# Windows of 64 nodes per octet, dst compared on two halves of the array, and 124 columns copied per octet in a graph-network kernel

## The chip, the cores and the metric

The kernel runs on one core of one Trainium2 chip. The metric is the device time of one execution in microseconds; the time of a version is the median of several runs. The profile is one execution taken by the hardware profiler. Its engines are PE (TensorE: matmuls; PEld is its weight load), DVE (VectorE), ACT (ScalarE), POOL (GpSimd) and SP (SyncE, which here only issues DMAs). Each engine runs its own instructions in order; they meet through semaphores.

## The reference

A message-passing layer on 12,500 nodes of 64 features and 400,000 edges, sorted by their target `dst`, followed by a residual and a layer norm. All arithmetic is float32.

```python
m_in = concatenate([x[src], x[dst], edge_attr])       # 64 + 64 + 16
h = silu(m_in @ W1 + b1)
messages = silu(h @ W2 + b2)
agg = segment_sum(messages, dst, num_segments=12500)
out = silu(concatenate([x, agg]) @ W3 + b3)
result = layernorm(x + out)
```

## The kernel before

**Tiles, octets, chunks.** The edges are cut into 3125 tiles of 128. Eight tiles make an octet (391 of them, the last with five tiles), three octets a chunk (131). The loop at L555 runs over octets and spreads each octet's work over several of its turns. Inside it the order of instructions on PE, ACT, DVE and SP is the order of the text (`manual_schedule`, L552); POOL has only the gathers.

**First layer.** The product `x @ W1[0:64]` is computed once for all nodes and written to the table `pa` in DRAM (`table`, L171, in turns 1 to 5 of the loop). The rows of `pa` for an octet's sources are gathered in three ways:

- by POOL's indirect DMA, one per tile of 128 edges (`gather`, L332, line L341), three octets ahead, into one of five buffers `ga`. The first nine octets (`RAW`) gather rows of `x` itself, because the table is not there yet;
- by copies of single columns. `x` transposed is resident in SBUF (`xs`, two copies on two halves of the partitions). For one pair of tiles in some octets (`pairs`), ACT and DVE copy 256 columns of 64 features one by one (`columns`, L244, line L267), each a copy of 64 x 4 bytes whose address is a register that was loaded from the list of sources. The copies are spread over the turns before: 56 per octet on ACT (`ACOLS`, two halves of 28, registers in loads of at most 16) and 48 on DVE (`VCOLS`, two halves of 24, one load each). 104 per octet replace a pair of tiles, two gathers, every 2.46 octets: 153 pairs in all;
- by single-row DMAs from SP (`rows`, L280), 16 per octet: 23 pairs.

The rest of the first layer uses that edges are sorted: the targets of a chunk lie in a window of 112 nodes from its first `dst` on. `window_load` (L346) reads these nodes' columns of `x`, `window_product` (L354) multiplies them with `W1[64:128]`, `window_copy` (L359) puts the result into rows 0 to 111 of the weights `xw`, whose last 16 rows hold the attributes' part of `W1`. `load` (L365) broadcasts an octet's `dst` to 112 partitions (`dr`) and loads the edges' attributes into the last 16 rows of `oh`; `compare_dst` (L377) writes into the first 112 rows of `oh` whether an edge's `dst` is the node of the row. One product of `xw` and `oh` (L401) so gives the target's and the attributes' part; even and odd tiles go to the two halves of the columns of the array. The gathered rows are added by products with the identity (L415), the copied columns by a product with `W1` (L412). ACT applies silu (L419).

**Second layer and sums.** `second_layer` (L422) multiplies with `W2` (L428 for the bias, L430) and applies silu (L434). `compare_nodes` (L385) makes, per tile, the matrix of which edge belongs to which of the 112 nodes, and `add_up` (L437) multiplies the messages with it (L443), accumulating over a chunk's 24 tiles in PSUM. `add_window` (L446) adds the sum to `agg` in SBUF, once a chunk.

**Nodes.** When the windows have passed a group of 512 nodes, `node_product` to `store` (L467 to L510) compute the output, spread over later turns by the table `todo`.

**Check.** After the loop (L612 to L635) DVE computes the distance of each `dst` from its window's base and whether any lies outside; if so, the slow version `general` runs. It does not for these inputs.

Of the kernel before, what the change touches and what calls it, by code (L numbers as in the profile page):

```python
# [20 lines left out]
P = 128  # L21
G = 4
CT = 24
OT = 8
W = 112
# [4 lines left out]
ACOLS = (28, 28)  # L30
VCOLS = (24, 24)
ROWS = 16
ALOAD = 16
XBASE = (0, 64 << 18)
XADDR = 35840
# [8 lines left out]
def kernel(  # L44
# [8 lines left out]
    attr_t: bass.AP,  # L53
    base: bass.AP,
# [31 lines left out]
    with ExitStack() as inner:  # L86
        windows(inner, tc, ident, badi, pa, x, xt, src_c, src_row, dst_c, dst_row, attr_t, base, w1, b1, w2, b2, w3, b3, out, edges)
# [7 lines left out]
def windows(ctx, tc, ident, badi, pa, x, xt, src_c, src_row, dst_c, dst_row, attr_t, base, w1, b1, w2, b2, w3, b3, out, edges):  # L95
# [5 lines left out]
    NCH = base.shape[1]  # L101
    assert W + A == P and N + W <= NP
# [15 lines left out]
    bi = fast.tile([1, NCH], I32, name="bi")  # L118
# [48 lines left out]
    def resident(s, c):  # L167
        w = min(XC, NP - c)
        nc.sync.dma_start(xs[s * D:(s + 1) * D, c:c + w], xt[:, c:c + w])
# [19 lines left out]
    bf = fast.tile([1, NCH], F32, name="bf")  # L189
    nc.vector.tensor_copy(bf, bi)  # L190
    rowi = fast.tile([P, W], I32, name="rowi")
    nc.gpsimd.iota(rowi, pattern=[[1, W]], base=0, channel_multiplier=0)
    row = fast.tile([P, W], F32, name="row")
    nc.vector.tensor_copy(row, rowi)
    coli = fast.tile([P, 1], I32, name="coli")
    nc.gpsimd.iota(coli, pattern=[[0, 1]], base=0, channel_multiplier=1)
    colf = fast.tile([P, 1], F32, name="colf")
    nc.vector.tensor_copy(colf, coli)

    wb = fast.tile([P, NCH], F32, name="wb")  # L200
    wps = ctx.enter_context(tc.tile_pool(name="wps", bufs=1, space=PSUM))
    wrow = wps.tile([P, 512], F32, name="wrow")
    wn = wrow[:, 3 * W:3 * W + NCH]
    assert 3 * W + NCH <= 512
    pb = mis.tile([P, NCH], F32, name="mm")
    nc.tensor.matmul(pb, ones, bf, start=True, stop=True)
    nc.vector.tensor_copy(wb, pb)
    nc.vector.tensor_scalar(wn, pb, colf, None, op0=OP.add)

    xw = []  # L210
    for k in range(3):
        t = fast.tile([P, D], F32, name=f"xw{k}")
        nc.sync.dma_start(t[W:P, :], w1[2 * D:2 * D + A, :])
        xw.append(t)

    octs = []
    for c in range(NCH):
        t1 = min(TILES, (c + 1) * CT)
        octs += [(c, t, min(OT, t1 - t), t == c * CT, t + OT >= t1) for t in range(c * CT, t1, OT)]

    with tc.tile_pool(name="gat", bufs=AHEAD + 2) as gat, tc.tile_pool(name="drp", bufs=2) as drp, \
            tc.tile_pool(name="hot", bufs=3) as hot, \
            tc.tile_pool(name="ehp", bufs=4) as ehp, \
            tc.tile_pool(name="work", bufs=2) as work, tc.tile_pool(name="win", bufs=2) as win, \
# [19 lines left out]
        def columns(o, eng, part):  # L244
# [3 lines left out]
            if eng == ENG.Activation:  # L248
                lo, n, copy = lo + sum(ACOLS[:part]), ACOLS[part], nc.scalar.copy
            else:  # L250
                lo, n, copy = lo + sum(ACOLS) + sum(VCOLS[:part]), VCOLS[part], nc.vector.tensor_copy
            hi = lo + n
            while lo < hi:
# [3 lines left out]
                n = min(hi - lo, P - e0 % P, ALOAD if eng == ENG.Activation else P)  # L257
# [8 lines left out]
                for e, r in zip(range(e0 % P, e0 % P + n), regs):  # L266
                    copy(t[h, 4 * e:4 * e + 4], xb[h, ds(r - (XBASE[s] + XADDR), 4)])  # L267
# [62 lines left out]
        sums = psa.tile([P, 2, W], F32, name="pg")  # L330
# [15 lines left out]
        def window_load(c):  # L346
            regs = nc.values_load(bi[0:1, c:c + 1], engines=(ENG.SP, ENG.DVE), min_val=0, max_val=N - 1,
                                  skip_runtime_bounds_check_because="dst names a node")
            winreg[c] = regs
            xr = win.tile([D, W], F32, name="xr")  # L350
            nc.sync.dma_start(xr, xt[:, ds(regs, W)])
            winrow[c] = xr

        def window_product(c):  # L354
            pw = mis.tile([P, D], F32, name="mm")
            nc.tensor.matmul(pw[0:W, :], winrow[c], w1ab[:, 1, :], start=True, stop=True)  # L356
            winrow[c] = pw

        def window_copy(c):  # L359
            nc.vector.tensor_copy(xw[c % 3][0:W, :], winrow[c][0:W, :])  # L360
            r = wrow[:, c % 3 * W:(c % 3 + 1) * W]
            nc.vector.tensor_scalar(r, row, wb[:, c:c + 1], None, op0=OP.add)
            winrow[c] = r

        def load(o):  # L365
            c, t0, n, first, last = octs[o]
            n2 = n + n % 2
            e = slice(t0 * P, (t0 + n2) * P)
            dr = drp.tile([W, OT * P], I32, name="dr")
            nc.sync.dma_start(dr[:, :n2 * P], dst_row[:, e].to_broadcast([W, n2 * P]))  # L370
            oh = hot.tile([P, OT * P], F32, name="oh")
            nc.sync.dma_start(oh[W:P, :n2 * P], attr_t[:, e])
            loaded[o] = dr, oh
# [3 lines left out]
        def compare_dst(o):  # L377
            c, t0, n, first, last = octs[o]
            n2 = n + n % 2
            dr, oh = loaded.pop(o)  # L380
            nc.vector.tensor_tensor(oh[0:W, :n2 * P], dr[:, :n2 * P], wn[0:W, c:c + 1].to_broadcast([W, n2 * P]),  # L381
                                    op=OP.is_equal)
            hots[o] = [oh]

        def compare_nodes(o):  # L385
            c, t0, n, first, last = octs[o]
            eh = ehp.tile([P, OT, W], F32, name="eh")
            nc.vector.tensor_tensor(eh[:, :n], winrow[c][:, None, :].to_broadcast([P, n, W]),  # L388
                                    dc[:, t0:t0 + n, None].to_broadcast([P, n, W]), op=OP.is_equal)
            hots[o].append(eh)  # L390

        def first_layer(o):
# [6 lines left out]
            ohv = oh.rearrange("p (i s e) -> p s i e", s=2, e=P)  # L399
            for s in range(2):  # L400
                nc.tensor.matmul(p1[s * D:(s + 1) * D, :k], xw[c % 3], ohv[:, s, :k], start=True, stop=False,  # L401
# [35 lines left out]
        def add_up(o):  # L437
            c, t0, n, first, last = octs[o]
            m, eh = made.pop(o)
            pg = sums[:, c % 2, :]  # L440
            for i in range(n):
                s = i % 2
                nc.tensor.matmul(pg[s * D:(s + 1) * D, :], m[:, i, :], eh[:, i, :],  # L443
                                 start=(first and i < 2), stop=(last and i >= n - 2), skip_group_check=True)

        def add_window(c):  # L446
            a = agg[:, ds(winreg[c], W)]
            nc.vector.tensor_tensor(a, a, sums[:, c % 2, :], op=OP.add)  # L448
# [8 lines left out]
        eps = nv.tile([P, 1], F32, name="eps")  # L457

# [59 lines left out]
        NO = len(octs)  # L518
# [8 lines left out]
        for q in range(early):  # L527
            o = lead[due[q]] + 2
# [3 lines left out]
            later(o + 1, node_stats, q)  # L532
        for q0 in range(0, rest, RB):
            o = lead[due[q0 + RB - 1]] + 2
            later(o + 2, root, q0, q0 + RB)
            later(o + 3, inverse, q0, q0 + RB)
            for r in range(RB):
                later(o + 3 + 2 * r, divide, q0 + r)
                later(o + 4 + 2 * r, store, q0 + r)
# [6 lines left out]
        load(0)  # L546
        load(1)
        tables = list(range(0, N, 4 * P))
        per = -(-len(tables) // TABLES)
        parts = list(range(0, NP, XC))  # L550

        with tc.manual_schedule(engines={ENG.PE, ENG.Activation, ENG.DVE, ENG.SP}):  # L552
            compare_dst(0)
            compare_nodes(0)
            for o in range(NO + 1):  # L555
# [9 lines left out]
                if o == 8:  # L565
                    nc.sync.dma_start(dc[:, SCT:], dst_c[:, SCT:])
# [12 lines left out]
                if o + 2 < NO:  # L579
                    load(o + 2)  # L580
                    if octs[o + 2][3]:
                        window_load(octs[o + 2][0])
# [3 lines left out]
                if o >= 3 and octs[o - 3][4]:  # L586
                    add_window(octs[o - 3][0])
# [316 lines left out]
```

## Time and profile before

| | |
|---|---|
| median of 3 runs | 3553.34 us (3553.28 to 3558.27) |
| profiled execution | 3555.16 us, span of its instructions 3553.3 us |
| span per octet | 9.09 us |
| mean TensorE clock granted | 0.752 of full |
| L341, gathers on POOL | 2701 from `pa`, 72 from `x` |
| L267, column copies | 21112 on ACT (188 ns each, overlapping), 18056 on DVE (204 ns) |
| DMA | 327 MB, 92 GB/s in the mean |

In the groups below a line reads: source line, engine, operation, output <- inputs by the program's names, shape, count | busy us, mean ns of one | idle us of the engine just before them, and what ended most of that idle time. "issue" is time for which the profile shows nothing that the engine waits for. A line of the timeline gives start and duration in us, engine, line, operation, and in brackets the idle time before it. A line of waits gives who waited for whom, us in total, times, and the longest.

### The profile page before, as it was taken

How to read it: one execution, taken by the hardware profiler on the slowest of the kernel's cores; microseconds unless marked ns; L12 is line 12 of the kernel's file. 1: busy time of each engine (PE TensorE's matmuls, PEld its weight loads, DVE VectorE, ACT ScalarE, POOL GpSimd, SP SyncE). 2: the span in 40 equal slices, each digit the busy share in tenths (PEclk: the TensorE clock that was granted, in tenths of full speed). 3: DMA queues.
4: the chain of work that ended last, by engine and by line, in shares of the span. 5: the costliest groups of instructions: out<-in, count | busy, mean ns of one | idle time of the engine just before them, and what ended most of it. 6: DMA issues, size and time to landing. Idle time of an engine off the chain costs nothing.

```text
span 3553.3 us, 96997 instructions
## 1 busy us (share of the span) xinstructions
PE 2717.1 (76%) x15387; PEld 1796.0 (51%) x15387; DVE 2551.0 (72%) x19955; ACT 2598.8 (73%) x21941; POOL 2659.2 (75%) x2782
## 2 busy tenths in 40 slices
PE   7877877777777778777777777777877777777786
PEld 5554554555545455455454554544544545545454
DVE  3667767777687677776777777777778777677673
ACT  1568777787787777777877777778778777777772
POOL 7677777777777777777777777777777777777774
PEclk7867777777777777777777777777677777777776
DMA  6433333333333333333333333333333333333331
GB/s 158 131 90 95 86 89 92 84 92 90 88 99 91 91 89 85 95 86 89 96 93 94 91 85 93 91 89 89 86 95 94 90 92 86 91 90 87 90 95 47
DMA packets 199259, 327.19 MB, mean 92 GB/s; under 512 B 94959, under 2 KB 103306, under 8 KB 197722
## 3 DMA queue, kind: packets, MB, share of 16 engines
q1 hardware_dynamic: 96142, 226.51, 20.3%
q0 software_dynamic: 88736, 91.04, 13.8%
q10 hardware_dynamic: 13740, 3.32, 0.4%
q14 instruction: 511, 4.19, 0.4%
q8 instruction: 130, 2.13, 0.3%
HBM read 314.20 MB, written 6.40 MB: 90 GB/s over the span
## 4 chain that ended last, share of the span: by engine, by line
POOL 50%; issue 20%; DMA 17%; PE 12%; ACT 1%; DVE 0%; SPq 0%; ACTq 0%; POOLq 0%; DVEq 0%
POOL ga L341 50%; DMA ga<-pa,sc 16%; PE p L430 3%; PE pg L443 2%; PE p L401 2%; PE p L415 1%; PE mm L177 1%; PE p L428 1%; ACT cx L267 1%; PE mm L477 1%; PE mm L476 1%; DMA ga<-in_x,sc 0%; PE p L410 0%; PE p L412 0%; PE mm L406 0%
## 5 line engine op out<-in xcount | busy, mean ns | idle before, releaser
L341 POOL DMA_INDIRECT ga<-pa,sc x2701 | 2589.9, 959 | 838.8 <-issue 746.9
L267 ACT COPY cx<-xs 64x4 uint8 x21112 | 2079.2, 188 | 216.8 <-issue 172.0
L267 DVE COPY cx<-xs 64x4 uint8 x18056 | 1458.6, 204 | 204.4 <-issue 172.7
L415 PE MATMUL p<-ident,ga 128*128 128x128 f32 x2702 | 616.8, 349 | 784.2 <-DMA ga<-pa,sc 781.4
L415 PEld LDWEIGHTS p<-ident,ga 128*128 128x128 f32 x2702 | 461.4, 233 | 1109.6 <-issue 945.6
L430 PE MATMUL p<-w2d,h 128*128 128x128 f32 x3126 | 621.9, 361 | 0.0
L419 ACT ACTIVATE h<-p,b1s 128x512 f32<-128x512 f32 x391 | 268.2, 686 | 480.6 <-PE p L415 437.4
L430 PEld LDWEIGHTS p<-w2d,h 128*128 128x128 f32 x3126 | 530.0, 256 | 127.0 <-issue 127.0
L401 PE MATMUL p<-oh,xw 128*64 128x512 f32 x1564 | 561.8, 806 | 5.5 <-DMA sc<-in_src_c 5.5
L388 DVE TENSOR_TENSOR eh<-wrow,dc 128x896 f32<-128x896 f32 x391 | 424.7, 1086 | 178.9 <-PE pg L443 165.3
L443 PE MATMUL pg<-eh,m 128*64 128x112 f32 x6250 | 528.5, 329 | 14.0 <-ACT m L434 13.9
L381 DVE TENSOR_TENSOR oh<-dr,wrow 112x1024 f32<-112x1024 int32 x391 | 473.1, 1210 | 28.2 <-DMA dr<-in_dst_row 16.8
L443 PEld LDWEIGHTS pg<-eh,m 128*64 128x64 f32 x6250 | 420.3, 178 | 83.5 <-issue 42.4
L434 ACT ACTIVATE m<-p 128x512 f32<-128x512 f32 x391 | 232.6, 595 | 116.2 <-PE p L430 83.0
L428 PE MATMUL p<-b2r,one 3*128 3x512 bf16 x391 | 190.3, 487 | 0.0
L360 DVE COPY xw<-mm 112x64 f32<-112x64 f32 x131 | 29.0, 222 | 208.5 <-PE mm L356 208.5
L448 DVE TENSOR_TENSOR agg<-agg,pg 128x112 f32 x131 | 35.0, 267 | 193.5 <-PE pg L443 184.8
L412 PEld LDWEIGHTS p<-cx,w1d 128*128 128x128 f32 x306 | 56.7, 233 | 188.6 <-issue 188.6
L401 PEld LDWEIGHTS p<-oh,xw 128*64 128x64 f32 x1564 | 94.0, 165 | 60.3 <-issue 23.7
L483 ACT ACTIVATE z<-mm 128x256 f32<-128x256 f32 (+1 forms) x25 | 9.6, 383 | 115.3 <-PE mm L477 115.3
L412 PE MATMUL p<-cx,w1d 128*128 128x128 f32 x306 | 91.3, 388 | 0.0
L341 POOL DMA_INDIRECT ga<-in_x,sc x72 | 68.1, 946 | 22.7 <-issue 20.6
(73 smaller groups left out, 790.2 us busy)
## 6 DMA issues: line engine op xcount, KB each, us to landing
dr<-in_dst_row SPq DMA_DIRECT2D x390, 448.0 KB
rx<-pa SPq DMA_DIRECT2D x5888, 0.2 KB
ga<-pa,sc POOLq DMA_INDIRECT x2701
oh<-in_attr_t SPq DMA_DIRECT2D x390, 64.0 KB
xs<-in_xt SPq DMA_DIRECT2D x12, 512.0 KB
xr<-in_xt SPq DMA_DIRECT2D x131, 28.0 KB
pa<-v ACTq DMA_DIRECT2D x24, 128.0 KB
xa<-in_x SPq DMA_DIRECT2D x24, 128.0 KB
```

What stands on the lines that cost most here:

```text
L267: copy(t[h, 4 * e:4 * e + 4], xb[h, ds(r - (XBASE[s] + XADDR), 4)])
L341: nc.gpsimd.indirect_dma_start(out=ga[:, i, :], out_offset=None, in_=x if o < RAW else pa[:, :], in_offset=bass.IndirectOffsetOnAxis(ap=sc ...
L381: nc.vector.tensor_tensor(oh[0:W, :n2 * P], dr[:, :n2 * P], wn[0:W, c:c + 1].to_broadcast([W, n2 * P]), op=OP.is_equal)
L388: nc.vector.tensor_tensor(eh[:, :n], winrow[c][:, None, :].to_broadcast([P, n, W]), dc[:, t0:t0 + n, None].to_broadcast([P, n, W]), op=OP. ...
L401: nc.tensor.matmul(p1[s * D:(s + 1) * D, :k], xw[c % 3], ohv[:, s, :k], start=True, stop=False, skip_group_check=True)
L412: nc.tensor.matmul(p1[:, 0, :], w1d, cols.pop(o), start=False, stop=False, skip_group_check=True)
L415: nc.tensor.matmul(p1[:, i, :], g2.rearrange("p s d -> p (s d)"), ident, start=False, stop=(i == k - 1), skip_group_check=True)
L419: nc.scalar.activation(h[:, :k], p1[:, :k], AF.Silu, bias=b1s)
L428: nc.tensor.matmul(p2[:, :n2, :], one3, b2r[:, :n2, :], start=True, stop=False, skip_group_check=True)
L430: nc.tensor.matmul(p2[:, 2 * i:2 * i + 2, :].rearrange("p s d -> p (s d)"), h[:, i, :], w2d, start=False, stop=(i == k - 1), skip_group_ch ...
L434: nc.scalar.activation(m[:, :n2], p2[:, :n2], AF.Silu)
L443: nc.tensor.matmul(pg[s * D:(s + 1) * D, :], m[:, i, :], eh[:, i, :], start=(first and i < 2), stop=(last and i >= n - 2), skip_group_chec ...
```

## The change

Each octet gets a window of its own, of 64 nodes for the first layer (`W`) and 48 for the sums (`S`). `base` holds the first `dst` of each octet. Window load, product, copy and add therefore run once per octet; the base registers are loaded for four octets at a time (`bases`); the product stands at the head of a turn, before the first layer, and the add one turn later than before. The product is written to both halves of the partitions, so `xw` holds the 64 nodes twice.

`dst` and attributes are arranged on the host (`dst_2`, `attr_2`): even tiles in the upper half of the partitions, odd tiles in the lower. `load` brings a chunk's `dst` with two broadcasts and its attributes with one DMA. `compare_dst` then runs over 128 partitions x 512 elements. The first layer's product is split: one product of the attributes (32 partitions) with the block-diagonal `w1c`, and two products of 64 x 64 quadrants of the array, even tiles on one, odd tiles on the other.

For the node compare, `dc` is turned in place into the distance from the octet's base (`relative`), in pieces during the loop; one row `row` of 0 to 47 serves all octets. The check's minimum and maximum are taken in ten pieces from turn 30 on; at the end only small steps are left, with `evi` written into `xs`.

Columns: ACT 32 and 28 per octet, DVE 32 and 32. Registers come in loads of 16 and then 8. DVE's copy is written as a `tensor_reduce` with maximum over one element. The resident copies of `x` and the late part of `dst` are loaded from ACT's queue instead of SP's.

```diff
-W = 112
+W = 64
+S = 48
-ACOLS = (28, 28)
-VCOLS = (24, 24)
+ACOLS = (32, 28)
+VCOLS = (32, 32)
-ALOAD = 16
+LOADS = (16, 8)
...
     def resident(s, c):
         w = min(XC, NP - c)
-        nc.sync.dma_start(xs[s * D:(s + 1) * D, c:c + w], xt[:, c:c + w])
+        nc.scalar.dma_start(xs[s * D:(s + 1) * D, c:c + w], xt[:, c:c + w])
...
+    rel = dc.bitcast(F32)
+
+    def relative(a, b):
+        f = b // OT * OT
+        if f > a:
+            nc.vector.tensor_tensor(rel[:, a:f].rearrange("p (c t) -> p c t", t=OT),
+                                    dc[:, a:f].rearrange("p (c t) -> p c t", t=OT),
+                                    wb[:, a // OT:f // OT, None].to_broadcast([P, (f - a) // OT, OT]), op=OP.subtract)
...
                 for e, r in zip(range(e0 % P, e0 % P + n), regs):
-                    copy(t[h, 4 * e:4 * e + 4], xb[h, ds(r - (XBASE[s] + XADDR), 4)])
+                    to, frm = t[h, 4 * e:4 * e + 4], xb[h, ds(r - (XBASE[s] + XADDR), 4)]
+                    if eng == ENG.DVE:
+                        nc.vector.tensor_reduce(to, frm[:, :, None], AX.X, OP.max)
+                    else:
+                        nc.scalar.copy(to, frm)
...
-        def window_product(c):
+        def window_product(o):
             pw = mis.tile([P, D], F32, name="mm")
-            nc.tensor.matmul(pw[0:W, :], winrow[c], w1ab[:, 1, :], start=True, stop=True)
-            winrow[c] = pw
+            for q in range(2):
+                nc.tensor.matmul(pw[q * W:(q + 1) * W, :], winrow[o], w1ab[:, 1, :], start=True, stop=True)
+            winrow[o] = pw
...
-            nc.vector.tensor_tensor(oh[0:W, :n2 * P], dr[:, :n2 * P], wn[0:W, c:c + 1].to_broadcast([W, n2 * P]),
-                                    op=OP.is_equal)
+            oh = hot.tile([P, OT // 2 * P], F32, name="oh")
+            e = o % 3 * OT // 2 * P
+            w = n2 // 2 * P
+            nc.vector.tensor_tensor(oh[:, :w], dr[:, e:e + w], wn[:, o:o + 1].to_broadcast([P, w]), op=OP.is_equal)
...
-            for s in range(2):
-                nc.tensor.matmul(p1[s * D:(s + 1) * D, :k], xw[c % 3], ohv[:, s, :k], start=True, stop=False,
+            h = slice(o % 3 * 2 * A, (o % 3 + 1) * 2 * A)
+            nc.tensor.matmul(p1[:, :k], w1c[h, :], loaded[c][1][h, :k * P], start=True, stop=False, skip_group_check=True)
+            for q in range(2):
+                h = slice(q * W, (q + 1) * W)
+                nc.tensor.matmul(p1[q * D:(q + 1) * D, :k], xw[o % 3][h, :], oh[h, :k * P], start=False, stop=False,
                                  skip_group_check=True)
...
-            pg = sums[:, c % 2, :]
+            pg = sums[:, o % 4, :]
             for i in range(n):
                 s = i % 2
                 nc.tensor.matmul(pg[s * D:(s + 1) * D, :], m[:, i, :], eh[:, i, :],
-                                 start=(first and i < 2), stop=(last and i >= n - 2), skip_group_check=True)
+                                 start=(i < 2), stop=(i >= n - 2), skip_group_check=True)
...
-                if o + 2 < NO:
-                    load(o + 2)
-                    if octs[o + 2][3]:
-                        window_load(octs[o + 2][0])
+                if o + 2 < NO and octs[o + 2][3] and o + 2:
+                    load(octs[o + 2][0])
+                if o + 3 < NO:
+                    window_load(o + 3)
+                if o + 1 < NO:
+                    window_product(o + 1)
                 if o + 1 < NO:
                     compare_dst(o + 1)
                 columns(o, ENG.DVE, 0)
-                if o >= 3 and octs[o - 3][4]:
-                    add_window(octs[o - 3][0])
+                if o >= 4:
+                    add_window(o - 4)
...
-        evi = nv.tile([P, NCH], I32, name="evi")
-        nc.gpsimd.iota(evi, pattern=[[STEP, NCH]], base=0, channel_multiplier=0)
-        lag = xs[:, TILES:TILES + NCH]
-        nc.vector.tensor_tensor(lag, evi, wb, op=OP.subtract)
+        evi = xs.bitcast(I32)[:, :3 * NCH]
+        nc.gpsimd.iota(evi, pattern=[[STEP, NCH], [0, 3]], base=0, channel_multiplier=0)
+        lag = xs[:, 3 * NCH:3 * NCH + NO]
+        nc.vector.tensor_tensor(lag, evi[:, :NO], wb, op=OP.subtract)
```

## The prediction

> **What bounds the kernel now.** I read the shares and the chain first, then the groups of instructions, then the timeline of a few microseconds in mid-kernel.
>
> ```profile
> span 3553.3 us, 96997 instructions
> PE 2717.1 (76%) x15387; PEld 1796.0 (51%) x15387; DVE 2551.0 (72%) x19955; ACT 2598.8 (73%) x21941; POOL 2659.2 (75%) x2782
> POOL 50%; issue 20%; DMA 17%; PE 12%; ACT 1%; DVE 0%; SPq 0%; ACTq 0%; POOLq 0%; DVEq 0%
> L341 POOL DMA_INDIRECT ga<-pa,sc x2701 | 2589.9, 959 | 838.8 <-issue 746.9
> PE p L415 <- DMA ga<-pa,sc: 781.4, 452, 5.9
> ```
>
> Four engines are 72 to 76% busy, so the shares name no bound; the chain does: POOL, the "issue" between its gathers and their landing make 87%. POOL waits for no other engine (its 838.8 us of idle time are almost all "issue"), while PE waits 781.4 us for gathers.
>
> ```profile
> 2001.99 0.94 POOL L341 DMA_INDIRECT ga<-pa,sc  x1 [0.30 <-issue]
> 2004.49 0.94 POOL L341 DMA_INDIRECT ga<-pa,sc  x1 [0.30 <-issue]
> 2007.94 1.97 DVE L267 COPY cx<-xs 64x4 uint8 x24
> 2009.49 1.25 POOL L341 DMA_INDIRECT ga<-pa,sc  x1 [0.30 <-issue]
> ...
> 3479.94 5.15 POOL L341 DMA_INDIRECT ga<-pa,sc  x1 [0.30 <-issue]
> 3480.87 3.40 DVE L614 TENSOR_TENSOR xs<-dc,wb 128x3120 f32<-128x3120 int32 x1
> 3494.22 3.40 DVE L624 TENSOR_REDUCE lim<-xs 128x1 f32<-128x3125 f32 x1
> 3495.43 0.94 POOL L341 DMA_INDIRECT ga<-pa,sc  x1 [0.30 <-issue]
> 3496.68 0.94 POOL L341 DMA_INDIRECT ga<-pa,sc  x1 [0.30 <-issue]
> ```
>
> A gather starts every 1.249 us (0.944 and 0.305 of issue). Some take longer: 2589.9 - 2701 x 0.944 = 40 us in all. Laying every gather over the DVE instructions under it, 35.6 us of that fall on gathers beside L267 copies (1682 gathers), 4.2 us on the one beside L614, 0.5 us on all others (1090). So DVE's column copies lengthen gathers; a 3.4 us reduction (L624) leaves them at 0.94. The whole time is then: start 2.8 + 2773 gathers x 1.249 = 3463.5 + lengthening 40.3 + 15.0 waiting once for the table pa at 93 to 108 us + 31.9 after the last gather = 3553.5 against a span of 3553.3. The profiled run took 3555.2, the median is 3553.3: sums against the span stand for the median.
>
> **The change on POOL.** ACT copies 60 columns per octet instead of 56, DVE 64 instead of 48: 124 for 104. A replaced pair is 256 columns, so pairs go from 153 to 183, and the gathers from 3125 - 306 - 46 = 2773 to 3125 - 366 - 46 = 2713. 60 x 1.249 = **-74.9 us**. An octet then lasts 2713 x 1.249 / 391 = **8.67 us** on POOL (before 9.09 of span); every other engine must stay below that for the gain to show.
>
> DVE's columns become reductions of one element each. If they behave as L624 and L625 do, the 35.6 us go; if they behave as copies do, 64 for 48 makes it 47. No row shows a 4-element reduction beside a gather; I take **-35**, ends -36 and +12. L614 leaves the end (-4.2); in its place nine subtractions of up to 368 columns with the same two operands (relative) stand in the loop, each some 0.5 us by L614's length: 0 to 1.2 us of gather each, I take +4. Sum **0**, ends -4 and +7.
>
> **The change on DVE**, per octet. The compare of dst has 512 columns: 1.211 us at 1024 and 0.944 at 768 give 0.68. The compare of nodes has 384: 1.087 at 896, 0.730 at 560 give 0.54. Window copy and window add come every octet: 0.22 and 0.20 (L360, L448); the row of L362 (0.33 per chunk) goes. Columns: 24 take 1.85 to 1.97 us, so 0.079 each: 64 x 0.079 = 5.06. Registers are fetched in three loads per half (16, 8, 8) instead of one: idle before copies is now 204.4/391 = 0.52 us, I double it to 1.0. Addresses and node statistics 0.3. Together **8.0** of 8.67: hidden behind POOL, with 0.67 to spare. The window copy now waits on PE each octet (L360 waited 208.5 us in 131 chunks, 1.6 each); behind it stand the node compare and 32 columns, for which PE asks an octet later. The product it waits for now stands ahead of the first layer, behind work for gathers two octets older, so this wait falls in the spare time.
>
> The Trainium skill (VectorE: DVE Perf Modes, Rules for kernel authors) speaks against this part: it calls tensor_reduce on a hot path the slowest operation, at single rate. The rows say how much: 3.40 us for 3125 elements of L624 and 3.40 for the 3120 of L614, so one element per 1.04 ns. At four elements that is 4 ns beside at most 2 for a double-rate copy: 64 x 2 ns = 0.13 us per octet, in the spare time. Read as a wholly slower operation, it decides only from 0.079 + 0.67/64 = 0.089 us each.
>
> **On ACT**: busy 2598.8/391 = 6.65 per octet, plus 4 copies x 0.109 (2079.2 + 216.8 over 21112) = 7.1, plus 0.44 of "issue" before copies (172.0/391): 7.5 to 7.8. Hidden. The resident loads and dst, 15 issues of 0.5 us, move from SP's queue into ACT's in the first nine octets; ACT waits there for PE 4 to 9 us at a time.
>
> **On PE**, per octet at the present mean clock of 0.75:
>
> ```profile
> L401 PE MATMUL p<-oh,xw 128*64 128x512 f32 x1564 | 561.8, 806 | 5.5 <-DMA sc<-in_src_c 5.5
> L443 PE MATMUL pg<-eh,m 128*64 128x112 f32 x6250 | 528.5, 329 | 14.0 <-ACT m L434 13.9
> L356 PE MATMUL mm<-w1ab,xr 64*112 64x64 f32 x262 | 63.6, 331 | 4.2 <-DMA xr<-in_xt 4.2
> L410 PE MATMUL p<-m,w1d 128*128 128x512 f32 x18 | 13.0, 810 | 12.5 <-DVE m L409 12.5
> 109.00:143.00 34.00, 28.24 (x209) 1.00 0.65 177
> ```
>
> Busy now 2717.1/391 = 6.95. The attributes become a product of their own over all 128 columns: two passes like L410, 2 x 0.72 = +1.44. The two halves of L401 (1.44 per octet) become two quadrants, taken at the same price because L401's halves overlap (806 ns each, 359 of own busy time). Sums over 48 instead of 112: 0.085 each falls to the weight load's 0.067 (L443 PEld 420.3/6250): 16 x 0.018 = -0.3. Window product each octet, twice: +0.6 (0.3 to 0.8 by L356). Sum **8.7**, as much as POOL's 8.67. That is at clock 0.75, with PE idle a quarter of the time; the last line above is the stretch of 109 to 143 us (columns: PE busy, granted clock, DMA share, GB/s), where PE catches up and waits little, and there the clock is 1.00. At 1.00 the sum is 6.5. I take PE as hidden.
>
> Here too a rule speaks against the change: the Trainium skill (TensorEngine Tiling (Array Packing), Gotcha 1: PSUM Pressure) says different row tiles cannot access the same PSUM bank at the same time. The quadrants are two row tiles, and p1 is one bank. L401's halves are column tiles, so no row shows the case. By the rule the quadrants run one after the other, +1.44: 10.2 at clock 0.75, 7.6 at 1.00. POOL stays the bound if the clock rises above 10.2 x 0.75 / 8.67 = 0.88. By the row the end is 3456 whatever the clock above 0.75; by the rule with a clock of 0.80, 9.5 per octet, some 380 x 0.85 = 320 us more.
>
> **SP and DMA**: dr is loaded per chunk in halves (768 KB for three octets against 3 x 448), xr is 16 KB per octet: about 70 MB less of 327. SP loses its 348 us of waits for oh buffers and issues about as much as before. Worth nothing: POOL waited for none of it.
>
> **Start.** The table is built in octets 1 to 5, PE nearly without a pause (busy 19.2 of 20 us at 45 to 65). Each of these iterations gains the attribute product (2.1 us at half clock, 1.1 at full) and 0.6 of window product, less 0.4 of sums: four or five times 1.3 to 2.3, and POOL's 15 us wait for the table grows by as much: **+7**, ends 0 and +12.
>
> **End.** The check's iota now writes into xs, behind the last gather in POOL's queue; DVE's subtraction of it stands ahead of the window copy of the last octet but one. So that octet's first layer, which began at 3512 (9 us before the last gather ended), waits until about 2 us after it, and the node product (5.7 us) falls behind it. Against that the two 3.4 us reductions leave the end. PE at half clock there gives +13, at full +3: **+8**.
>
> **Sum**: 3553.3 - 74.9 - 35 + 0 + 7 + 8 = **3458 us**.
>
> **Rivals.**
> (a) POOL stays the bound but reductions lengthen gathers as copies did: 3458 + 35 = 3493, with more columns up to 3505. For it: only long reductions have been seen beside gathers. Chance 0.08.
> (b) DVE, ACT or PE comes level with POOL and part of the gain is lost to mutual waits: DVE 8.0 and PE 8.7 are close. A reduction of 0.092 us instead of 0.079 gives 8.0 + 0.83 = 8.83 per octet, 60 us more: 3480 to 3545. Chance 0.15.
> (c) Slower: the quadrants run one after the other and PE becomes the bound in every octet. It decides below a clock of 0.88 and is slower than before below 10.2 x 0.75 / 9.09 = 0.84; at 0.80 it ends near 3780. For it: the rule above, and that PE stayed at half clock from 45 to 65 us though busy 96% of it. Against: from 109 to 143 us, with these same matmuls, it had full clock. Chance 0.10.
> My forecast (POOL keeps its step, gathers at 0.94) has 0.66, own range 3435 to 3480.
>
> **Chances and range.** Measurement tells about 0.2% (7 us) from no change. Faster 0.89, same 0.01, slower 0.10. From 3430 (start and end cost nothing) to 3520 it leaves out all of (c), a third of (b), and 0.03 below: 0.18.
>
> **What would show it.** 2713 gathers, mean near 0.945 us, still ended by "issue"; columns as reductions at or below 0.079 us apart; PE's wait for gathers smaller but there, its clock above 0.75; wait for the table 20 to 27 us; 35 to 45 us after the last gather. Wrong if POOL shows waits for PE (buffers of ga not free), or gathers stay at 0.96.

## The result

The changed kernel takes 3567.64 us in the median (3564.75 to 3576.18), the kernel before, run beside it, 3555.28 us: a ratio of 1.0039, 95% interval 1.0026 to 1.0052. It is slower by 12 us; the prediction said 3458 us, faster by 95.

The profiled execution took 3568.47 us. The page of the changed kernel (busy us, share of the span, instructions; and the group of gathers):

```profile
span 3566.2 us, 112877 instructions
PE 3067.3 (86%) x17471; PEld 1818.5 (51%) x17471; DVE 2505.3 (70%) x26548; ACT 2723.2 (76%) x23509; POOL 2566.7 (72%) x2722
L363 POOL DMA_INDIRECT ga<-pa,sc x2641 | 2496.4, 945 | 936.9 <-issue 703.8
```

The gathers did what was forecast: there are 2641 + 72, and one from `pa` takes 945 ns. But of POOL's 936.9 us of idle time before them, "issue" no longer explains nearly all. The waits of the changed kernel (who waited for whom: us in total, times, longest):

```profile
PE pg L477 <- DVE xw L391: 441.5, 173, 7.3
DVE oh L414 <- DMA dr<-in_dst: 185.3, 87, 4.4
POOL ga L363 <- PE p L449: 121.5, 82, 6.9
POOL ga L363 <- DMA pa<-v: 35.4, 1, 35.4
```

POOL waits for PE to have read a `ga` buffer, which it did nowhere before. Laid out as in the prediction: start 2.7 + 2713 gathers x 1.249 = 3388.5 + lengthening 3.5 + the wait for the table 35.1 + 96.5 in 36 waits for `ga` buffers + 40.4 after the last gather = 3566.7, against a span of 3566.2. (The 121.5 us of the row include the usual 0.3 us of issue ahead of each such gather; 96.5 is what goes beyond it.) So the 109 us that are missing against the forecast are 96.5 us of waits that had been put at nothing, and 13 us at the start (35 us of table wait for 22).

Who is late? The row of sums, L477, says that PE waits for DVE; DVE waits for `dst`; PE itself is 86% busy. All three were suspected first (theories A, B and C below), and none of the three was the cause. The one engine that has no row on the page, SP, which only issues DMAs, was. Its waits in mid-kernel, 1500 to 3300 us (SPq is SP as the issuer of DMAs), before:

```profile
SPq L372 <- PE p L401: 156.8, 46, 10.3
SPq L372 <- PE p L415: 7.6, 23, 0.5
SPq L292 <- DMA dr<-in_dst_row: 7.0, 17, 0.8
```

and in the changed kernel:

```profile
SPq L314 <- DMA dr<-in_dst: 45.3, 60, 1.6
SPq L314 <- DMA at<-in_attr: 23.1, 53, 1.3
SPq L381 <- PE p L449: 14.3, 36, 1.1
SPq L314 <- DMA xr<-in_xt: 6.4, 14, 1.3
```

Before, SP's queue stood still for up to 10.3 us until PE had freed a buffer: it was ahead and had time to spare. After, its longest waits are for its own transfers, at most 1.6 us. Those that are put down to PE are none: no pause of 0.1 us stands ahead of these issues, PE's signal only falls inside the issue, and an issue with such a signal takes as long as one without (0.51 and 0.50 us in the mean). Three turns of SP in the changed kernel's timeline (start, us, engine, line, operation):

```profile
2006.79 5.10 SPq L314 DMA_DIRECT2D rx<-pa  x16
2011.94 0.36 SPq L501 DMA_DIRECT2D xa<-in_x  x1
2012.40 1.13 SPq L401 DMA_DIRECT2D dr<-in_dst  x2
2013.65 0.51 SPq L403 DMA_DIRECT2D at<-in_attr  x1
2015.34 0.53 SPq L381 DMA_DIRECT2D xr<-in_xt  x1
2017.02 5.58 SPq L314 DMA_DIRECT2D rx<-pa  x16
2022.73 0.23 SPq L341 DMA_DIRECT2D cxi<-in_src_row  x1
2023.19 0.49 SPq L381 DMA_DIRECT2D xr<-in_xt  x1
2025.27 5.07 SPq L314 DMA_DIRECT2D rx<-pa  x16
```

Each starts where the one before it ends; the holes of 1.2 and 1.6 us ahead of L314 at 2017.02 and 2025.27 are the loads of 16 registers for the rows (L310, median 1.416 us), that ahead of L381 at 2015.34 is mostly a load of four window bases (L371, 0.56 us). Adding up every instruction of SP between 1500 and 3300 us, per octet:

| per octet, us | instructions | gaps under 0.1 us between them | own transfers and unexplained | waits for other engines | sum = pace of the octets |
|---|---|---|---|---|---|
| before | 6.57 | 1.39 | 0.17 | 0.78 | 8.91 |
| changed | 6.99 | 1.43 | 0.54 | under 0.01 | 8.96 |

The four columns are all of SP's time, so that their sum is the pace by construction; what they tell is the last column. (The pace is 1800 us over the turns counted in them, and one turn more or less is 0.04 us; from turn 30 to turn 350 it is 8.91 before and 8.93 changed.)

POOL's own work is 8.67 us an octet. SP needs 8.93 to 8.96 and waits for nobody: it sets the pace, 0.26 to 0.29 us an octet too slow. How that reaches POOL late and by a detour: `ga` has five buffers, so POOL may run ahead. From PE's last read of a `ga` buffer to the gather that fills it again there were some 32 us in the mean before, all through the run; in the changed kernel this reserve has shrunk to the bare 0.3 us of issue between octets 64 and 80, and from then on each delay of the chain (SP's `dst` or window load late, DVE's compare, PE's products, the buffer) arrives at POOL. As an estimate, 0.26 to 0.29 x 391 = 102 to 113 us, less the reserve of 17 us that octets 14 to 29 have in the mean, is 85 to 96 us; 96.5 were measured.

The runs listed below the table of experiments were made where the kernel before itself took 4879 to 5000 us (in the trace of `e1_add_first` instructions of SP, DVE and ACT come in stretches at steps of 0.71 us; why is not known), so that they tell nothing about 3567.6 us.

### The profile page after: what moved, and what is told of

It is laid out like the page before. It is cut to its first block, busy times and chain, and to the rows that moved or that the text cites. A ratio compares the mean times of both kernels' runs of the same rounds, so it can differ in the third digit from the quotient of the medians.

```text
span 3566.2 us, 112877 instructions
## 1 busy us (share of the span) xinstructions
PE 3067.3 (86%) x17471; PEld 1818.5 (51%) x17471; DVE 2505.3 (70%) x26548; ACT 2723.2 (76%) x23509; POOL 2566.7 (72%) x2722
## 5 line engine op out<-in xcount | busy, mean ns | idle before, releaser
L363 POOL DMA_INDIRECT ga<-pa,sc x2641 | 2496.4, 945 | 936.9 <-issue 703.8
L289 ACT COPY cx<-xs 64x4 uint8 x22680 | 2228.1, 188 | 142.1 <-issue 109.0
L287 DVE TENSOR_REDUCE cx<-xs 64x4 uint8 x24168 | 1791.6, 150 | 590.1 <-issue 532.4
L477 PE MATMUL pg<-eh,m 128*64 128x48 f32 x6250 | 321.1, 255 | 460.0 <-DVE xw L391 441.5
L432 PE MATMUL p<-at,w1c 32*128 32x512 f32 (+1 forms) x782 | 609.5, 869 | 0.0
L435 PE MATMUL p<-oh,xw 64*64 64x512 f32 x1564 | 582.5, 832 | 0.0
L477 PEld LDWEIGHTS pg<-eh,m 128*64 128x64 f32 x6250 | 272.8, 167 | 528.2 <-issue 325.2
L414 DVE TENSOR_TENSOR oh<-dr,wrow 128x512 f32<-128x512 int32 x391 | 265.0, 678 | 207.6 <-DMA dr<-in_dst 185.3
L435 PEld LDWEIGHTS p<-oh,xw 64*64 64x64 f32 x1564 | 93.4, 163 | 431.4 <-issue 319.6
L420 DVE TENSOR_TENSOR eh<-wrow,dc 128x384 f32<-128x384 f32 x391 | 212.8, 544 | 0.2
L387 PE MATMUL mm<-w1ab,xr 64*64 64x64 f32 x1564 | 156.6, 287 | 16.1 <-DMA xr<-in_xt 16.1
L432 PEld LDWEIGHTS p<-at,w1c 32*128 32x128 f32 x782 | 150.8, 239 | 35.4
```

The source lines that it names most:

```text
L287: nc.vector.tensor_reduce(to, frm[:, :, None], AX.X, OP.max)
L289: nc.scalar.copy(to, frm)
L363: nc.gpsimd.indirect_dma_start(out=ga[:, i, :], out_offset=None, in_=x if o < RAW else pa[:, :], in_offset=bass.IndirectOffsetOnAxis(ap=sc ...
L387: nc.tensor.matmul(pw[q * W:(q + 1) * W, :], winrow[o], w1ab[:, 1, :], start=True, stop=True)
L414: nc.vector.tensor_tensor(oh[:, :w], dr[:, e:e + w], wn[:, o:o + 1].to_broadcast([P, w]), op=OP.is_equal)
L432: nc.tensor.matmul(p1[:, :k], w1c[h, :], loaded[c][1][h, :k * P], start=True, stop=False, skip_group_check=True)
```

## The experiments

Each is compared with the kernel before on the same chip (3552.7 to 3559.3 us in the runs that are read; the changed kernel stands at 1.0039). "Waits for `ga`" is POOL's idle time beyond the 0.3 us of issue, the table wait at the start apart. "SP per octet" is SP's time without its waits for other engines: where it equals the pace, SP waits for nobody.

| run | us (lowest to highest) | ratio, 95% interval | waits for `ga`, us | SP per octet / pace, us |
|---|---|---|---|---|
| `e11_add_first_again` | 3538.1 (3524.3 to 3549.6) | 0.9949 (0.9931 to 0.9966) | 60 | 8.86 / 8.87 |
| `e5_both` | 3541.6 (3522.3 to 3551.6) | 0.9950 (0.9926 to 0.9974) | 65 | 8.91 / 8.91 |
| `e12_no_attr_again` | 3505.6 (3503.5 to 3509.6) | 0.9858 (0.9841 to 0.9874) | 64 | 8.87 / 8.87 |
| `e9_one_product` | 3447.9 (3446.6 to 3449.6) | 0.9693 (0.9677 to 0.9709) | 0 | 8.66 / 8.65 |
| `e10_one_product_only` | 3452.0 (3448.2 to 3456.4) | 0.9712 (0.9693 to 0.9730) | 7 | 8.73 / 8.74 |
| `e14_no_attr_add_first` | 3504.0 (3502.5 to 3511.5) | 0.9866 (0.9848 to 0.9885) | 51 | 8.86 / 8.87 |
| `e6_copies` | 3581.5 (3569.9 to 3589.4) | 1.0075 (1.0052 to 1.0098) | 27 | 8.88 / 8.91 |
| `e8_one_more_ga_again` | 3574.4 (3568.2 to 3587.4) | 1.0063 (1.0039 to 1.0086) | 92 | 8.95 / 8.96 |
| `e19_no_attr_dst_early` | 3500.9 (3499.4 to 3505.8) | 0.9842 (0.9826 to 0.9859) | 64 | 8.87 / 8.87 |
| `e20_eight_rows` | 3497.0 (3489.0 to 3510.2) | 0.9816 (0.9795 to 0.9838) | 0 | 5.7 and 3.0 of waiting / 8.70 |

Beside 4879 to 5000 us for the kernel before: `e1_add_first` 5351.0, `e2_no_attr` 5252.6, `e3_dst_early` 5376.3 and again 5368.1, `e8_one_more_ga` 5415.4, `e15_no_attr_dst_early` 5233.1 and 5165.1 as `e18_no_attr_dst_early`, `e16_no_attr_48_rows` 5261.1: each 5 to 8% slower than the kernel before there. The kernels of `e1`, `e2`, `e8` and `e15` are those of e11, e12, the second e8 and e19.

**Theory A: PE's sums wait for DVE's add.** In the row of 441.5 us L477's first matmul waits, by the trace, until 146 ns after `add_window` of two octets before. The add stands behind the compare and 32 columns; it is moved to the head of the turn:

```diff
+                if o >= 4:
+                    add_window(o - 4)
                 if o + 1 < NO:
                     compare_dst(o + 1)
                 columns(o, ENG.DVE, 0)
-                if o >= 4:
-                    add_window(o - 4)
```

> The same kernel as e1_add_first, run again because in that run the kernel before itself took 4999.9 us, so that nothing could be told against 3567.6 us. The vector engine's add of the sums stands at the head of its turn. Theory A (TensorE's sums wait for that add, and ga buffers come free late): the 441.5 us of sums that the trace puts down to the window copy fall below 100 us, GpSimd's waits for ga buffers fall from 96.5 us to below 30, and the time falls to 3490 to 3510 us. Theory B (TensorE's own added products fill it): the waits stay within 30 us, 3550 to 3570 us. Theory C (late dst loads hold the vector engine): 3555 to 3570 us.

Measured 3538.1 us, neither theory's number. The row `PE pg L477 <- DVE xw L391` disappears from the head of the list, but new ones come: 212.1 us of L477 for the add and 267.2 us of L435's weight loads for the window copy. 60 us of POOL's waits stay. The wait moved, which suggests that what is late lies behind DVE.

**Theory C: late loads of `dst`.** DVE waits 185.3 us for them. With the add moved as above, they are issued an octet earlier:

```diff
-                if o + 2 < NO and octs[o + 2][3] and o + 2:
-                    load(octs[o + 2][0])
+                if o + 3 < NO and octs[o + 3][3]:
+                    load(octs[o + 3][0])
```

> The add at the head of the vector engine's turn, and in addition each chunk's dst and attributes loaded one octet earlier. Theory A alone: within 5 us of e11_add_first_again, since what the loads cost is only passed on through the add. Theory C (the loads hold the vector engine, 185 us of its waits): a further fall of 20 to 60 us below e11_add_first_again, to 3460 to 3490 us, and no wait over 1 us of the compare of dst for its load. Theory B: as changed, 3550 to 3570 us.

3541.6 us, as without it. That is what theory A alone forecast for this step, though its own number had failed in e11. DVE waits 62.7 us for `dst` instead of 202.7, and PE now waits 331.5 us for the window load `xr`, which stands behind `dst` in SP's queue (e11: 76.2). Here what comes earlier in that queue makes something else later.

**Theory B: PE is full.** The attributes' product is the largest thing that the change added to PE.

```diff
-            nc.tensor.matmul(p1[:, :k], w1c[h, :], loaded[c][1][h, :k * P], start=True, stop=False, skip_group_check=True)
```

> The same kernel as e2_no_attr: the attributes' product is left out (the result lacks the attributes' part), the rest as changed; 1.56 us of TensorE an octet go. Theory B (TensorE full): GpSimd's waits for ga buffers fall below 20 us and the time to 3480 to 3500 us. Theory A (the sums wait for the vector engine): TensorE only waits longer for the vector engine, the sums' wait grows from 441.5 us by 200 or more, and the time stays above 3530 us.

3505.6 us. PE's busy time falls from 3067.3 to 2521.5 us, less than before the change (2717.1), and still POOL waits 64 us:

```profile
PE pg L476 <- DVE xw L391: 870.9, 320, 8.2
POOL ga L363 <- PE p L448: 75.6, 42, 5.9
```

PE waits twice as long at the sums, as theory A forecast for its waits; the time fits neither theory. So PE's work is not what holds POOL in mid-kernel. Of the 62 us, 29 are gained at the start (see below), and the pace falls by 0.09 us an octet, 35 us. SP's waits for its own transfers fall by 0.10 us (0.44 for 0.54); why is open.

Both at once, the product left out and the add moved:

> The attributes' product left out (the result lacks the attributes' part) and the vector engine's add at the head of its turn; the dst loads stay late. Theory A+B (both loops are lifted, so GpSimd sets the time): 3445 to 3465 us, GpSimd's waits for ga buffers below 10 us after the first 150 us, and at any time some 25 us or more between the end of TensorE's reading of a ga buffer and the gather that fills it again. If the late loads (theory C) are a third loop at the same height: 3480 to 3505 us, with the compare of dst still waiting 150 us and more for its load and gathers waiting in their train.

3504.0 us and 51 us of waits: nothing is gained over e12, as forecast for the case that theory C's late loads hold too. DVE's wait for `dst` stands at 228.3 us. The product left out and the loads early:

> The same kernel as e15_no_attr_dst_early, once more, for the same reason. The attributes' product is left out (the result lacks the attributes' part), and dst is loaded one octet earlier. Theory B+C: 3445 to 3470 us, and waits for ga buffers below 15 us after the first 150 us. If what e10_one_product_only gained lay in the one product's form: 3495 to 3515 us.

3500.9 us, not the 3445 to 3470 of theory B+C. Its waits show the queue again:

```profile
PE mm L387 <- DMA xr<-in_xt: 461.6, 137, 11.4
DVE oh L414 <- DMA dr<-in_dst: 203.0, 93, 5.1
POOL ga L363 <- PE p L448: 82.8, 62, 6.1
```

Loaded earlier, `dst` is as late as ever, and the window load is late too. Theories A and B fall singly, and A, B and C fall in these pairs; C alone has no run that can be read (the loads early as the only edit, below).

**One product for the whole first layer.** A version written to beat both kernels: window and attributes in one product of 128 x 128 (48 nodes for each half block by block in rows 0 to 95, the attributes' weights in the last 32), so that `dst` goes to 2 x 48 rows instead of 2 x 64 and the attributes straight into `oh`; and the two moves above.

```diff
-            for q in range(2):
-                h = slice(q * W, (q + 1) * W)
-                nc.tensor.matmul(p1[q * D:(q + 1) * D, :k], xw[o % 3][h, :], oh[h, :k * P], start=False, ...
+            nc.tensor.matmul(p1[:, :k], xw[o % 3], oh[:, :k * P], start=True, stop=False, skip_group_check=True)
...
-                nc.sync.dma_start(dr[k * W:(k + 1) * W, e], dst_2[k:k + 1, d].to_broadcast([W, e.stop - e.start]))
+                nc.sync.dma_start(dr[k * S:(k + 1) * S, e], dst_2[k:k + 1, d].to_broadcast([S, e.stop - e.start]))
...
-            nc.sync.dma_start(xr, xt[:, ds(winreg.pop((ENG.SP, o)), W)])
+            nc.sync.dma_start(xr, xt[:, None, ds(winreg.pop((ENG.SP, o)), S)].to_broadcast([D, 2, S]))
...
-            nc.vector.tensor_copy(xw[o % 3], winrow.pop(o))
+            nc.vector.tensor_tensor(xw[o % 3][0:2 * S, :].rearrange("p (h d) -> p h d", h=2),
+                                    winrow.pop(o)[0:2 * S, None, :].to_broadcast([2 * S, 2, D]), mask, op=OP.mult)
```

> A version meant to beat both: the first layer's window and attributes in one product of 128 rows by 128 columns (window of 48 nodes for each half, block by block, the attributes' weights in the last 32 rows), the add at the head of the vector engine's turn, and the loads one octet earlier. TensorE loses some 1.5 us an octet against the changed kernel. Theory A: some 5 us below e5_both, no more, since GpSimd sets the time once the add no longer holds the sums: 3460 to 3490 us. Theory B: 3460 to 3480 us, 80 us and more below e5_both. If GpSimd's gathers lengthen or the longer vector multiply holds the window, above 3500 us.

3447.9 us, the fastest of all and 12 us below the lowest number forecast, and POOL waits for no `ga` buffer. The same without the two moves:

> The first layer in one product of 128 rows by 128 columns, as in e9_one_product, and nothing else against the changed kernel: the vector engine's add and the loads stand where the change put them. Theory A+B (two loops stood level above GpSimd's 8.67 us an octet: TensorE's own work, and TensorE and the vector engine waiting for each other through the add; each alone still holds GpSimd): as e12_no_attr_again, 3495 to 3515 us, with 40 to 80 us of GpSimd's waits for ga buffers left and the sums waiting for the vector engine 600 us or more. Theory B alone (only TensorE's added work): as e9_one_product, 3445 to 3455 us, and no wait for ga buffers after the first 150 us.

3452.0 us: the restructuring does it alone. "Theory B alone" forecast this number, but e12 had taken as much from PE (busy 2521.5 us; e10: 2522.6) and kept 64 us of waits, so PE's time cannot be the reason. SP's queue is: one of the two `dst` transfers of a chunk is issued in 388 ns on average instead of 547 (e12: 555), the attributes' in 437 instead of 546 (e12: 674), the window load costs 632 instead of 505, and SP waits 0.34 us an octet for its own transfers instead of 0.54 (e12: 0.44). In sum 8.73 us an octet for e12's 8.87. 0.14 x 391 is some 55 us; e12 and e10 lie 54 us apart. And 8.73 is still above 8.67: in e10 the reserve ahead of POOL shrinks from 31 us to 0.3 through the whole run, and the first waits come at 3039 us. It lives on its reserve to the end. The faster e9, where SP's 8.66 us stand level with POOL's 8.67, keeps its reserve of 31 us and gains only 4 us more. SP has no spare time in e9 either.

**Is the end POOL's work at all?** DVE's columns as copies again, one line:

```diff
-                        nc.vector.tensor_reduce(to, frm[:, :, None], AX.X, OP.max)
+                        nc.vector.tensor_copy(to, frm)
```

> Only this differs from the changed kernel: the vector engine's columns are copied, as in the kernel before, not reduced, so that its gathers should lengthen by some 35 us again (0.945 to about 0.958 us each). If the loop of TensorE and the vector engine sets the end, as theory A+B says, the lengthening is taken out of GpSimd's waits for ga buffers (96.5 to about 60 us) and the time stays within 12 us of 3567.6. If GpSimd's own work still sets the end and its waits only come on top, the time grows by 30 to 40 us, to about 3603 us.

The gathers lengthen (the groups of gathers and of DVE's columns in this kernel):

```profile
L363 POOL DMA_INDIRECT ga<-pa,sc x2641 | 2568.6, 973 | 873.0 <-issue 714.3
L287 DVE COPY cx<-xs 64x4 uint8 x24168 | 2036.4, 198 | 392.5 <-issue 336.7
```

2568.6 for 2496.4 us, 72 us more, twice what was expected; the time grows by 14 us (1.0075 for 1.0039), and the waits for `ga` shrink from 96.5 to 27 us. What POOL does more it waits less; the rest of the growth lies at the start and the end (in the profiled run 5.6 us more of table wait, 9.5 us more after the last gather). POOL doesn't set the pace of the changed kernel.

**Single late turns or a pace?** 67 of the 96.5 us of waits fall within 20 us after a turn with node products, so that a deeper queue might ride them out: six `ga` buffers (`bufs=AHEAD + 3`).

> Six ga buffers in place of five, all else as changed (the same kernel as e8_one_more_ga). If TensorE's loop is slower than GpSimd for the whole run, a further buffer is used up once: GpSimd may run one octet further ahead, its waits fall by some 9 us, and the time falls by 0 to 9 us, to 3558 to 3568. If the waits are single late turns (the turns with node products) that a deeper queue would ride out, they nearly all go: below 25 us of waits, 3490 to 3510 us.

3574.4 us, no gain at all, 6 us above the range forecast for a pace. The reserve starts at 31 us instead of 17 and is gone by 1116 us of the run: a pace that is too slow uses up a larger reserve too. (13 us more stand after the last gather, 53.2 for 40.4.)

**Theory D: SP's queue.** Formed only then, from the tally of SP's instructions in the table above: in e5, e11, e12, e14 and e19, SP waits for other engines 0.01 us an octet or less, as in the changed kernel. The test takes work from SP and gives some to POOL: 8 rows per octet copied by SP instead of 16.

```diff
-ROWS = 16
+ROWS = 8
```

> Only this differs from the changed kernel: SyncE copies 8 rows of the table for each octet in place of 16, so that its rows fill a pair every 32 octets instead of every 16, and GpSimd has 24 gathers more (2737). TensorE, the vector engine and the scalar engine do as before. Theory D (SyncE's queue sets the end: in the changed kernel's trace it is taken up for 8.96 of 8.96 us an octet by its own issues, its register loads and waits for its own transfers, and waits for no engine): SyncE falls to some 6.3 us an octet and GpSimd sets the time with more gathers: 2.8 + 2737 x 1.249 + 3.5 + 15 to 35 at the start + 40 at the end, 3480 to 3500 us, and the waits for ga buffers fall from 96.5 us below 15. Theories A, B and C (TensorE's own work, the add, or where the loads stand set the end): no less than 3560 us, and waits for ga buffers of 70 us or more.

3497.0 us, ratio 0.9816 (0.9795 to 0.9838): inside the range of D, 63 us outside that of the others. POOL has 24 gathers more than in the changed kernel and the time falls by some 70 us. PE's products, the add and the place of the loads are those of the changed kernel, so that the run speaks against C alone as well. SP's waits between 1500 and 3300 us, and the group of gathers, in this kernel:

```profile
SPq L341 <- ACTq L280: 463.6, 94, 12.7
SPq L381 <- PE mm L387: 97.3, 33, 15.8
SPq L314 <- DMA dr<-in_dst: 62.5, 64, 1.9
```
```profile
L363 POOL DMA_INDIRECT ga<-pa,sc x2665 | 2518.8, 945 | 853.3 <-issue 714.7 <-DMA ga<-pa,sc 70.4 <-DMA pa<-v 41.4
```

SP again waits for others, up to 15.8 us; POOL's idle time is "issue" and landing again, with no wait for PE beyond the usual 0.3 us. PE does all that the changed kernel's PE does (88% busy) and is hidden: its reserve ahead of POOL's gathers is 25 to 31 us in the mean from octet 53 on. The run lays out as 2.8 + 2737 x 1.249 = 3418.5 + 3.3 + 41.1 at the start + 43.7 at the end = 3509.4, its span 3508.5. The wait at the start is longer than the 15 to 35 us forecast. The edit halves the rows' issues and their transfers together: it shows the queue as the bound, not how much of that is issuing and how much is waiting for its own transfers.

Two kernels have no time beside 3555 us: `dst` early as the only edit, and a quarter less of `dst` with the product left out.

> The same kernel as e3_dst_early: each chunk's dst and attributes loaded one octet earlier, all else as changed. Theory B+C (TensorE's added products and the late dst loads are two loops at about the same height, above GpSimd's 8.67 us an octet): with the loads early TensorE's loop still holds, so the time falls by no more than 35 us, to 3530 to 3570 us, though the compare of dst waits less than 90 us for its loads, after 185. Were the late loads the one cause, it would fall to 3450 to 3480 us.

> The attributes' product left out (the result lacks the attributes' part), and after the first two chunks dst loaded into 48 rows of each half in place of 64 (a quarter less), as in e10_one_product_only, so that the products contract 48 rows each; loads stay where they are in the order. Theory B+C: the loads land sooner, the compare of dst waits 100 to 180 us for them after 233, and the time falls from 3505.6 us towards 3452, to 3455 to 3490. If the size of the loads doesn't matter: 3495 to 3515 us.

Beside 4976.5 us for the kernel before they took 5368.1 and 5261.1 us (ratios 1.0775 and 1.0569). So the share of the smaller `dst` transfers alone in e10's gain is not measured. Also open is why SP waits for its own transfers 0.54 us an octet in the changed kernel, 0.44 to 0.51 in e5, e11, e12, e14 and e19, and 0.17 before.

## Why the prediction was wrong, by its steps

**POOL.** Right. 60 gathers fewer, and DVE's reductions leave the gathers alone: lengthening 40.3 us before, 3.5 after, and 75.9 with copies of 64 columns (e6). The forecast took -35 and named +12 as the other end; the copies would have made +36. The Trainium skill (SBUF — State Buffer, Who interferes with whom) has this rule: on trn2 `tensor_reduce` never takes the ports shared with GpSimd, a copy can. Both runs agree with it. These 72 us were earned on an engine that no longer set the end.

**DVE.** Right in size: busy 2505.3 us and 532.4 of "issue" make 7.8 us an octet (forecast 8.0), a reduction 1791.6/24168 = 0.074 us (0.079). The rule that reductions are slow decided nothing. (The 1.04 ns an element that the forecast read from 3.40 us for 3125 elements are 1.09; it changes nothing.)

**ACT.** 2723.2/391 = 6.96 us busy plus 109.0/391 = 0.28 of issue: 7.2 (forecast 7.5 to 7.8), hidden.

**PE.** Hidden, as taken, but not for the reason given. The groups of the attributes' product and of the quadrants in the changed kernel:

```profile
L432 PE MATMUL p<-at,w1c 32*128 32x512 f32 (+1 forms) x782 | 609.5, 869 | 0.0
L435 PE MATMUL p<-oh,xw 64*64 64x512 f32 x1564 | 582.5, 832 | 0.0
```

1.56 and 1.49 us an octet for 1.44 each. The quadrants cost what the halves of L401 cost (562 us), though they are two row tiles writing one bank, and in the trace the two start 7 ns apart, as L401's halves do; the rule of the Trainium skill (TensorEngine Tiling (Array Packing), Gotcha 1: PSUM Pressure) would have made it 1.44 more, and isn't seen. The sum 8.7 was too high (3067.3/391 = 7.85, with the same mean clock of 0.74), and the clock did not rise with the load: 0.742 after, 0.752 before. PE was hidden because 7.85 is below 8.67, as e20 shows.

**SP and DMA: the step that failed.** "SP loses its 348 us of waits for oh buffers and issues about as much as before. Worth nothing: POOL waited for none of it." SP was never given a sum, though every other engine was. The row, before, over the whole run:

```profile
SPq L372 <- PE p L401: 348.3, 105, 14.4
```

These 348.3 us (0.89 an octet) were not a cost that goes, they were nearly all the spare time that SP had: 9.09 - 0.89 = 8.2 us an octet of work, with 8.67 as the new limit. Onto that came, per octet: the window load every octet instead of every third, and its registers every fourth, +0.36; the 16-register load of the rows, from 1.10 to 1.31 us, +0.2; `dst` and attributes -0.16; waits for its own transfers, from 0.17 to 0.54, +0.37. Together 8.96. The row transfers alone, 16 x 0.32 us with the gaps between, were the larger half all along. The forecast saved 70 MB of transfers and looked at bytes; what counted was the time that the issues, the register loads and the waits for its own transfers take up in the queue. The forecast put this term at nothing; it was worth 96.5 us.

**Start.** Mis-sized: +20 for +7. PE builds the table there, and from 92 to 128 us it is busy nearly without a pause in both kernels. Columns: PE, PEld, DVE, ACT, POOL busy, granted clock, DMA share, GB/s; before, then after:

```profile
92.00:128.00 36.00, 32.66 (x204) 21.77 (x204) 15.57 (x36) 5.14 (x8) 15.81 (x18) 0.86 0.68 179
```
```profile
92.00:128.00 36.00, 34.44 (x151) 26.05 (x149) 8.28 (x20) 1.97 (x3) 0.62 (x2) 0.50 0.42 93
```

The forecast counted the added products; the clock granted in this stretch is 0.50 instead of 0.86. The table's own matmuls show it too: their median from 92 to 128 us is 272 ns before (L177) and 418 in the changed kernel (L180). That it belongs to PE's added product is shown by the runs without it or with one product (e9, e10, e12, e14, e19: table wait 6.1 to 13.0 us), against 21.3 to 41.1 us in the six that keep it. Why the clock falls just there was not tried. In e20, with 41.1 us, the mean reads 0.67, but its first clock record comes only at 101 us, and the median of its table matmuls from 40 to 128 us is 417 ns.

**End.** 40.4 us after the last gather, 40 forecast.

**Rivals.** (a) fell. (b) had the right shape, an engine that comes level and mutual waits, and named DVE, ACT and PE; SP was left out of the list, and its range of 3480 to 3545 was missed as well. (c), the only one on the slower side, did not happen; the slower time came about by a mechanism that had been given no chance. "Wrong if POOL shows waits for PE" did point to the place, not to the cause.

## What to carry to other kernels

Give every queue a sum per turn, those that only issue DMAs too: so many issues, register loads and waits, beside the limit that the change sets; the page has no busy row for such a queue, and here its long waits for others were its spare time. When a wait moves from engine to engine as each is relieved (441.5 us of sums, then 267.2 us for the window copy, then 461.6 us for a load), look for what they all wait behind, and see whether that engine waits for anyone itself. Test a suspected bound by giving the other engine more work: here 72 us more of gathers cost 14, and 24 gathers more with half of SP's rows gained 70.

## What the runs showed that was not expected

- The issue of one row DMA of 256 bytes holds SP for 0.23 us, 0.32 with its register move and gaps; a load of 16 registers 1.31 us on average (1.10 before, with the same 16).
- A `dst` broadcast of 6 KB to 48 rows is issued in 388 ns on average (e10), to 64 rows in 547 ns. The number of rows alone does not explain it: before, 4 KB to 112 rows took 331 ns.
- A reduction of 4 elements (0.074 us apart) costs DVE less than a copy of 4 (0.084, e6: 2036.4/24168), besides leaving the gathers alone.
- Five `ga` buffers hid a pace 0.26 to 0.29 us an octet too slow until 703 us of the run (the first wait for one); in e10 a pace less than 0.1 us too slow stayed hidden until 3039 us.
